# Second graph convolution: gathers a chunk ahead, loads behind the picks, node work in smaller steps

## Chip, cores and metric

The kernel runs on one core of a Trainium2 chip, in one launch. The metric is the device time of an execution in microseconds. Five runs before the change gave 1869.61 to 1880.85 us, median 1875.18.

The engines, with the names that the profile uses: TensorE is PE (its weight loads are PEld), VectorE is DVE, ScalarE is ACT, GpSimd is POOL, SyncE is SP. Each engine works through its own queue of instructions in order; they meet at semaphores.

## What is computed

Two graph layers over 6250 nodes and 100000 edges, which arrive sorted by destination. The first is a two-step graph convolution (GCN), the second an attention layer; behind each stands a residual sum and a layer norm.

```python
def gcn_conv(x, src, dst, ew, W, b):
    deg = segment_sum(ew, dst); dinv = where(deg > 0, rsqrt(deg), 0)
    norm = dinv[src] * ew * dinv[dst]
    h = x @ W
    return segment_sum(h[src] * norm[:, None], dst) + b
...
h = relu(gcn_conv(x, src, dst, ew, W1, b1))      # with self-loops
h = sigmoid(gcn_conv(h, src, dst, ew, W2, b2))   # the second convolution
x = layernorm(x + h)
...
z = x @ fc_w.T
e = leaky(z[src] @ aw[0] + z[dst] @ aw[1] + (r_h @ fc_r_w.T) @ aw[2])
alpha = softmax of e over the edges of a destination
out = relu(segment_sum(alpha * (z[src] + r_h @ fc_r_w.T), dst) + z @ loop_w)
x = layernorm(x + out)
```

The change touches the stage that computes the second convolution. The same stage finishes the first layer for nodes whose sums are complete, prepares what the attention layer needs of them, and computes the part of the scores that comes from the edges' features.

## The kernel before

The edges are cut into 49 chunks of 2048. Since edges are sorted, the destinations of a chunk lie in a window of 144 nodes, and each chunk advances by about 128 nodes. A chunk's source rows come in two ways. For most of them, 12 groups of rows, `pick` copies rows of a table held on chip (`hot`, in three bf16 parts) with matmuls by a 0/1 mask (L513), and ACT scales the result into `got` (L520). For the rest, 5 groups, POOL starts one indirect DMA each from the table `g2` in memory into `far` (L524). By a manual dependency (L527) a gather waits until the second of the three groups of picks is done. `sum_masks` builds `wm`, the 0/1 matrices that send rows to nodes of the window: DVE writes them for the picked rows (L545) and a small `fb` for the gathered ones (L551), which ACT scales (L560). `scatter` (L569) multiplies all 17 groups with them into one window in PSUM, and `add_in` (L574) has DVE add it into the accumulator `acc2`.

The loop over the chunks (L1157 to L1170) stands under a manual schedule, so each engine gets its instructions in the order in which the program writes them. In round c, SP is given the mask of chunk c + 2 (`load_mask`, L1049, 384 KB, three buffers) and the edge features of chunk c + 1 (`load_chunk`, L964, 768 KB, two buffers); then come the picks of c, its gathers and masks, the scatter of chunk c - 1, the product and sum over the features of chunk c on DVE (`dots_of`, L953 and L954), and the sum of chunk c - 1's window. Loads on SP wait in order, each for its buffer.

Between these stand two places in a round for node work (`pieces.go(ready, 1)`): one behind the masks, one behind `dots_of`. A piece is four blocks of 128 nodes, `x1_of`, a generator that stops at every `yield`; a piece begins when the chunks have passed its nodes. Its steps before the change are: product with `dinv` (L337) and sigmoid (L413); transposes (L417) and sum into `xt` (L419); statistics (L384, L385) and root (L388); reciprocals (L390, L391), norm on ACT (L394) and a store; transposes back (L427) and copy to `x1T` (L428); product with `wfT` (L436), copies to `zrows` (L439) and `asd` (L440) and a store; product with `wfl` (L444) and copies (L445, L449); three parts on DVE (L452 to L454) and a store. That is eight steps, two a round, so a piece fills four rounds. `Pieces` issues the next piece's loads (`xt`, `dr`) when a piece begins. The tiles `mm` in PSUM, which the node work's matmuls write, have two buffers, and they are shared with `row_work`, a second generator that prepares index rows for the attention layer and moves one step a round (L1166).

Of the kernel before, what the change touches and what calls it, by code (L numbers as in the profile page):

```python
# [31 lines left out]
GS = 5  # L32
# [8 lines left out]
def gnn_kernel(ctx, tc, x, src, dst, ea, ew, W1, b1, W2, b2, fcw, fcrw, attn, loopw, out):  # L41
# [11 lines left out]
    nc = tc.nc  # L53
    N, D = x.shape
# [13 lines left out]
    NC = CF + 1  # L68
    assert 9 <= NC <= 64

    batches, c0 = [], 0
    while c0 < NC:
        n = min((2, 5)[len(batches)] if len(batches) < 2 else 7, NC - c0)
# [3 lines left out]
    GP = N // P // 4  # L77
# [23 lines left out]
    edges = ctx.enter_context(ExitStack())  # L101
# [5 lines left out]
    g2 = dram.tile([N, D], F32, name="g2")  # L107
# [4 lines left out]
    masks = dram.tile([NC, P, GP * P], BF16, name="masks")  # L112
# [53 lines left out]
    behind = const.tile([P, P], F32, name="behind")  # L166
# [50 lines left out]
    last = keep.tile([P, NT, P], BF16, name="last")  # L217
# [178 lines left out]
    def whole(some, b0):  # L396

        n = sum(nb == P for _, nb in some)
        return [(P, slice(0, n))] * (n > 0) + [(some[-1][1], slice(n, n + 1))] * (n < len(some))

    def x1_of(acc, b0, n, xp, pool, to_hot):


        some = blocks[b0 : b0 + n]
        w = sum(nb for _, nb in some)
        at = slice(b0 * P, b0 * P + w)
        xt = xp.tile([P, 4, D], F32, name="xt")
        load_some(nc.sync, xt, x, b0, n)
        scale = by_dinv(acc, b0, n, xp)
        next(scale)  # L410
        yield
        next(scale, None)
        nc.scalar.activation(acc[:, at], acc[:, at], AF.Sigmoid, bias=cols[:, 1:2])  # L413
        yield
        ps = pool.tile([P, 4, D], F32, name="mm")
        for b, nb in some:
            nc.tensor.transpose(ps[:nb, b - b0, :], acc[:, b * P : b * P + nb], ident)  # L417
        for p, k in whole(some, b0):
            nc.vector.tensor_add(xt[:p, k, :], xt[:p, k, :], ps[:p, k, :])  # L419
        yield  # L420
        yield from normed(xt, some, b0, xp)
        store_blocks(nc.sync, x1d, xt, b0, n)
        yield
        x1T = xp.tile([P, 512], F32, name="x1T")
        ps = pool.tile([P, 512], F32, name="mm")
        for b, nb in some:
            nc.tensor.transpose(ps[:, (b - b0) * P : (b - b0) * P + nb], xt[:nb, b - b0, :], ident[:nb, :nb])  # L427
        nc.scalar.copy(x1T[:, :w], ps[:, :w])  # L428
        yield
        st = xp.tile([P, 4, D], F32, name="zrows")  # L430
        for k0 in range(0, len(some), 2):
            two = some[k0 : k0 + 2]
            ps = pool.tile([P, 2, D + 2], F32, name="mm")
            for b, nb in two:
                k = b - b0 - k0
                nc.tensor.matmul(ps[:nb, k, :], x1T[:, (b - b0) * P : (b - b0) * P + nb], wfT, start=True, stop=True)  # L436
            for p, k in whole(two, b0 + k0):
                to = slice(k0 + k.start, k0 + k.stop)
                nc.scalar.copy(st[:p, to, :], ps[:p, k, :D])  # L439
                nc.vector.tensor_copy(asd[:p, b0 + to.start : b0 + to.stop, :], ps[:p, k, D:])  # L440
        store_blocks(nc.sync, zd, st, b0, n)
        yield
        ps = pool.tile([P, 512], F32, name="mm")
        nc.tensor.matmul(ps[:, :w], wfl, x1T[:, :w], start=True, stop=True)  # L444
        nc.scalar.copy(acc[:, at], ps[:, :w])  # L445
        if to_hot and b0 < BP:
            m = min(n, BP - b0)
            part = xp.tile([P, 4, 3, D], BF16, name="part", bufs=1)
            nc.scalar.copy(part[:, :m, 0, :], st[:, :m])  # L449
            yield  # L450
            left = xp.tile([P, 4, D], F32, name="low")[:, :m]
            nc.vector.tensor_sub(left, st[:, :m], part[:, :m, 0, :])  # L452
            nc.vector.tensor_copy(part[:, :m, 1, :], left)
            nc.vector.tensor_sub(part[:, :m, 2, :], left, part[:, :m, 1, :])  # L454
            nc.sync.dma_start(hz[:, b0 : b0 + m], part[:, :m])
# [45 lines left out]
            while left:  # L501
                left = [piece for piece in left if next(piece, self) is not self]

    def pick(c, mask, hot, table, ps_g, wp, gots=4, fars=12):

        rows = []
        for g0 in range(0, GP, 4):
            n = min(4, GP - g0)
            ps = ps_g.tile([P, 4, D], F32, name="g")
            for g in range(n):  # L510
                for k in range(3):
                    for q in range(4):
                        picked = nc.tensor.matmul(ps[32 * q : 32 * q + 32, g, :],  # L513
                                         mask[:, (g0 + g) * P + 32 * q : (g0 + g) * P + 32 * q + 32],
                                         hot[:, 4 * (g0 + g) + q, k, :], start=k == 0, stop=k == 2)
            if g0 + 8 <= GP:
                most = picked
            got = wp.tile([P, 4, D], F32, name="got", bufs=gots)
            for g in range(n):
                nc.scalar.activation(got[:, g, :], ps[:, g, :], AF.Copy, scale=swt[:, c, g0 + g : g0 + g + 1])  # L520
            rows += [got[:, g, :] for g in range(n)]
        for g in range(GS):
            got = wp.tile([P, D], F32, name="far", bufs=fars)
            brought = nc.gpsimd.indirect_dma_start(  # L524
                out=got, out_offset=None, in_=table[:, :],
                in_offset=bass.IndirectOffsetOnAxis(ap=sidx[:, c, g : g + 1], axis=0))
            tc.add_manual_dep(brought.ins, most.ins.name,  # L527
                              mybir.DependencyInfo(mybir.DependencyClass.Sync, mybir.DependencyReason.DATA),
                              reason="rows by DMA behind most of a chunk's picks")
            rows.append(got)  # L530
        return rows

    def sum_masks(c, wp, halved=True, nears=2):

# [37 lines left out]
    def add_in(acc, c, ps):  # L572
        at = cbase_of(c)
        nc.vector.tensor_add(acc[:, ds(at, WC)], acc[:, ds(at, WC)], ps)  # L574
# [9 lines left out]
    with tc.tile_pool(name="prep", bufs=1) as prep, tc.tile_pool(name="ps_p", bufs=3, space=PSUM) as ps_mm, \  # L584
# [115 lines left out]
        ps = ps_mm.tile([P, 4, D], F32, name="mm")  # L700
# [12 lines left out]
    hot = hotp.enter_context(tc.tile_pool(name="hot", bufs=1)).tile([P, BP, 3, D], BF16, name="hot")  # L713
# [4 lines left out]
    sorts, c0 = [], 0  # L718
    while c0 < NC:
        n = min((3, 4)[len(sorts)] if len(sorts) < 2 else BATCH, NC - c0)  # L720
# [187 lines left out]
    with tc.tile_pool(name="xs0", bufs=1) as xp, tc.tile_pool(name="ps_d", bufs=3, space=PSUM) as ps_mm, \  # L908
# [8 lines left out]
        with tc.high_priority():  # L917
            for c0 in range(0, NC, 7):
                n = min(7, NC - c0)
# [3 lines left out]
                for c in range(c0, c0 + n):  # L923
                    m = ms[:, c - c0]
                    ps = ps_w.tile([3, WC], F32, name="win")
# [10 lines left out]
            ps = ps_w.tile([P, NB], F32, name="win")  # L936
# [16 lines left out]
            nc.vector.tensor_mul(part, part, ar_row[:p, None, None, :].to_broadcast([p, *part.shape[1:]]))  # L953
            nc.vector.tensor_reduce(dots[:p, c : c + m, ts], part, AX.X, OP.add)  # L954

    def load_edges(et, c0, n, ts):

        for c in range(c0, c0 + n) if c0 + n > CF else [c0]:
            m = 1 if c0 + n > CF else n
            cuts = [(0, P)] if c < CF else [(0, 96), (96, crem // TC)]  # L960
            for p0, p1 in cuts:
                of = ea[c * CC : min((c + m) * CC, c * CC + (p1 * TC if c == CF else m * CC)), :]
                of = of.rearrange("(c p t) f -> p c t f", c=m, t=TC)
                nc.sync.dma_start(et[p0:p1, c - c0 : c - c0 + m], of[p0:p1, :, ts, :])  # L964

    def early_dots(pool):

# [75 lines left out]
    kp = first.enter_context(tc.tile_pool(name="slots2", bufs=3))  # L1043
    slots_of = {}

    def load_mask(c):
        if c < NC:
            slots_of[c] = kp.tile([P, GP * P], BF16, name="mask")
            nc.sync.dma_start(slots_of[c], masks[c])  # L1049

    load_mask(0)
    load_mask(1)
    ap_ = edge_rows.enter_context(tc.tile_pool(name="arp", bufs=2))
    ets = {}

    def load_chunk(c):
        if c < NC:
            ets[c] = ap_.tile([P, 1, TL, D], F32, name="et")
            load_edges(ets[c], c, 1, slice(0, TL))

    load_chunk(0)
    with tc.tile_pool(name="tab2", bufs=2) as wp, tc.tile_pool(name="ps_t", bufs=3, space=PSUM) as ps_mm:
# [7 lines left out]
    with tc.tile_pool(name="conv2", bufs=2) as wp, tc.tile_pool(name="rows2", bufs=1) as rp, tc.tile_pool(name="x1p", bufs=2) as xp, \  # L1070
# [79 lines left out]
        rows_of = row_work()  # L1150

        nc.gpsimd.memset(asd, 0.0)
        pieces = Pieces(lambda b0, n: x1_of(acc2, b0, n, xp, ps_mm, True))
        held = None

        with tc.manual_schedule():
            for c in range(NC):  # L1157
                ready = lows[max(c - 1, 0)]
                load_mask(c + 2)
                load_chunk(c + 1)  # L1160
                new = pick(c, slots_of.pop(c), hot, g2, ps_g, wp, 6), sum_masks(c, wp, halved=False)
                pieces.go(ready, 1)
                if held is not None:
                    win = scatter(held, ps_w)
                dots_of(ets.pop(c), c, 1, slice(0, TL))
                next(rows_of, None)  # L1166
                pieces.go(ready, 1)
                if held is not None:
                    add_in(acc2, c - 1, win)
                held = new  # L1170
            for _ in rows_of:
                pass
            load_mask(0)
            load_mask(1)
            add_in(acc2, NC - 1, scatter(held, ps_w))
            pieces.finish()
# [473 lines left out]
```

## Time and profile before

| | us |
|---|---|
| median of five runs | 1875.18 |
| the profiled execution | 1876.59 |
| its span | 1874.7 |
| PE busy (matmuls) | 1509.3 (81% of the span) |
| DVE busy | 1409.0 (75%) |
| ACT busy | 1111.5 (59%) |
| POOL busy | 912.4 (49%) |

The span is the time from the first to the last instruction that the profiler recorded. A table of groups gives, for each line, engine and operation, its busy time and the mean of one; a table of waits says for which engine and line an instruction waited, with the total, how often and the longest. "issue" there means that the engine waited for nothing that the profile shows. In a timeline a row is a start, a duration, the engine, the line, the operation with its tiles and a count of merged instructions; in brackets stands the idle time before it and what ended it. The granted clock of PE, a share of full speed, was 0.908 over the profiled execution. Since neighbouring instructions overlap in the pipelines, a busy PE is not necessarily at its peak.

### The profile page before, as it was taken

The numbers are of one execution on the slowest core, as the hardware profiler recorded it, in microseconds if no ns is written. First come the engines' busy times: TensorE is split into PE (matmuls) and PEld (weight loads), VectorE is DVE, ScalarE is ACT, GpSimd is POOL, SyncE is SP. The second block draws the span as 40 slices with busy tenths as digits, with TensorE's granted clock in tenths as the row PEclk, the third lists the DMA queues.
The fourth block names the chain that finished last, engine by engine and source line by source line (L and its number), as shares of the span: only waits on it lengthen the run. The fifth ranks groups of instructions, "written<-read, shape, count | busy, mean of one in ns | idle before, by whom it ended". The sixth has DMA issues, their size and how long they took to land.

```text
span 1874.7 us, 77963 instructions
## 1 busy us (share of the span) xinstructions
PE 1509.3 (81%) x33767; PEld 1376.4 (73%) x33767; DVE 1409.0 (75%) x2979; ACT 1111.5 (59%) x3537; POOL 912.4 (49%) x951
## 2 busy tenths in 40 slices
PE   2866888989998777888989986578888788888996
PEld 1554787888997657777878875467778777788885
DVE  7695878887776578877887874788887777877552
ACT  1135565667788654667767764235666656667774
POOL 4023454566576447766776762114334344344552
PEclk9987999999998868899999997569999999999998
DMA  2112333344458666666776675655667567676663
GB/s 61 42 38 85 100 112 101 108 131 135 135 156 262 198 188 188 196 208 203 225 236 197 214 218 177 188 146 158 206 169 219 156 187 195 181 205 171 178 199 72
DMA packets 261369, 306.86 MB, mean 164 GB/s; under 512 B 38387, under 2 KB 193785, under 8 KB 260212
## 3 DMA queue, kind: packets, MB, share of 16 engines
q1 hardware_dynamic: 229311, 244.90, 41.5%
q0 software_dynamic: 23520, 48.22, 12.4%
q10 hardware_dynamic: 8184, 8.65, 1.4%
q8 instruction: 267, 4.37, 1.0%
q14 instruction: 87, 0.71, 0.1%
HBM read 260.42 MB, written 41.25 MB: 161 GB/s over the span
## 4 chain that ended last, share of the span: by engine, by line
PE 26%; DMA 12%; DVE 11%; issue 7%; POOL 6%; ACT 3%; SPq 0%; DVEq 0%; POOLq 0%; ACTq 0%
PE win L569 11%; POOL far L524 6%; PE g L513 6%; DMA rk<-srow 4%; DMA far<-g,sidx 4%; PE r L1414 2%; PE k L1267 2%; DMA al<-shd 2%; DVE sel L1270 1%; PE mm L362 1%; ACT got L520 1%; DVE wb L265 1%; DVE ohm L265 1%; PE rec L1431 1%; DVE asr L1271 1%
## 5 line engine op out<-in xcount | busy, mean ns | idle before, releaser
L524 POOL DMA_INDIRECT far<-g,sidx x490 | 581.5, 1187 | 332.7 <-PE g L513 174.2
L520 ACT ACTIVATE got<-g,swt 128x128 f32<-128x128 f32 x1764 | 484.2, 386 | 249.2 <-PE g L513 196.5
L569 PE MATMUL win<-wm,got 128*128 128x144 f32 x3528 | 499.6, 300 | 11.8 <-issue 9.6
L569 PEld LDWEIGHTS win<-wm,got 128*128 128x128 f32 x3528 | 472.1, 200 | 28.4 <-issue 21.7
L524 POOL DMA_INDIRECT far<-zd,sidx x245 | 268.1, 1094 | 440.1 <-PE g L513 346.6
L513 PE MATMUL g<-hot,mask 128*32 128x128 bf16 x21168 | 373.8, 228 | 67.3 <-issue 58.8
L513 PEld LDWEIGHTS <-mask 128*32 128x32 bf16 x21168 | 326.9, 101 | 95.4 <-issue 80.5
L560 ACT ACTIVATE wm<-fb,swt 128x64 f32<-128x64 bf16 (+1 forms) x735 | 198.7, 384 | 43.7 <-DVE swt L1386 28.2
L569 PE MATMUL win<-wm,far 128*128 128x64 f32 (+1 forms) x1470 | 186.4, 272 | 29.0 <-DMA far<-g,sidx 29.0
L569 PEld LDWEIGHTS win<-wm,far 128*128 128x128 f32 x1470 | 181.4, 194 | 31.5 <-issue 21.7
L543 ACT CAST wm<-wb 128x864 f32<-128x864 bf16 x196 | 177.4, 953 | 23.5 <-PE win L569 18.7
L1267 PE MATMUL k<-adp,rk 128*128 128x49 bf16 x2352 | 89.7, 194 | 53.2 <-DVE sel L1270 46.9
L574 DVE TENSOR_TENSOR acc<-acc,win 128x144 f32 x147 | 44.4, 302 | 115.0 <-PE win L569 105.0
L1267 PEld LDWEIGHTS <-rk 128*128 128x128 bf16 x2352 | 83.1, 103 | 62.8 <-issue 51.2
L265 DVE TENSOR_TENSOR ohm<-iotab,pm 128x2048 bf16<-128x2048 bf16 x98 | 118.9, 1213 | 1.6 <-PE rec L849 1.5
L265 DVE TENSOR_TENSOR wb<-iota,sdst 128x1728 bf16<-128x1728 bf16 x98 | 103.0, 1051 | 19.4 <-ACT wm L543 19.3
L351 POOL TENSOR_TENSOR hot<-low,hot 128x512 bf16<-128x512 f32 x24 | 37.4, 1558 | 136.0 <-DVE hot L350 123.6
L545 DVE TENSOR_TENSOR wm<-iota,sdst 128x1728 f32<-128x1728 f32 x49 | 95.6, 1951 | 1.1 <-POOL hot L351 1.1
L954 DVE TENSOR_REDUCE dots<-et 128x12 f32<-128x1536 f32 (+1 forms) x49 | 85.9, 1753 | 1.7
L953 DVE TENSOR_TENSOR et<-et,ar_row 128x1536 f32<-128x1536 f32 (+1 forms) x49 | 85.6, 1747 | 0.0
L1259 DVE TENSOR_SCALAR rk<-rk,iotap 128x1024 bf16<-128x1024 bf16 x98 | 48.1, 494 | 36.5 <-DMA rk<-srow 36.2
L1262 ACT COPY blk<-blks 128x16 bf16<-128x16 bf16 x98 | 19.5, 207 | 92.9 <-DVE ohb L265 89.1
(401 smaller groups left out, 2259.9 us busy)
## 6 DMA issues: line engine op xcount, KB each, us to landing
et<-in_edge_attr_dram SPq DMA_DIRECT2D x97, 512.0 KB
mask<-masks SPq DMA_DIRECT2D x98, 384.0 KB
et<-in_edge_attr_dram SPq DMA_DIRECT2D x48, 768.0 KB
rk<-srow SPq DMA_DIRECT2D x98, 256.0 KB
mask<-srd SPq DMA_DIRECT2D x49, 384.0 KB
masks<-mask SPq DMA_DIRECT2D x49, 384.0 KB
ee<-in_edge_attr_dram SPq DMA_DIRECT2D x24, 512.0 KB
far<-g,sidx POOLq DMA_INDIRECT x490
```

Of the source, the lines that this page charges most:

```text
L265: nc.vector.tensor_tensor(out.rearrange("p t (h d) -> p t h d", d=2), row[:, None].to_broadcast(some), of[:, :, None, :].to_broadcast(some ...
L513: picked = nc.tensor.matmul(ps[32 * q : 32 * q + 32, g, :], mask[:, (g0 + g) * P + 32 * q : (g0 + g) * P + 32 * q + 32], hot[:, 4 * (g0 + ...
L520: nc.scalar.activation(got[:, g, :], ps[:, g, :], AF.Copy, scale=swt[:, c, g0 + g : g0 + g + 1])
L524: brought = nc.gpsimd.indirect_dma_start(out=got, out_offset=None, in_=table[:, :], in_offset=bass.IndirectOffsetOnAxis(ap=sidx[:, c, g : ...
L543: nc.scalar.copy(wm[:, n0 : n0 + half], wb[:, n0 : n0 + half])
L545: nc.vector.tensor_tensor(wm[:, :NEAR].rearrange("p (g w) -> p g w", w=WC), iota[:, None, 1 : WC + 1].to_broadcast([P, GP, WC]), sdst[:, c ...
L560: nc.scalar.activation(m, b, AF.Copy, scale=swt[:, c, GP + g : GP + g + 1])
L569: nc.tensor.matmul(ps[:, n0 : n0 + m.shape[-1]], row, m, start=g == 0, stop=g == len(rows) - 1)
L953: nc.vector.tensor_mul(part, part, ar_row[:p, None, None, :].to_broadcast([p, *part.shape[1:]]))
L954: nc.vector.tensor_reduce(dots[:p, c : c + m, ts], part, AX.X, OP.add)
L1259: nc.vector.tensor_scalar(mk, mk, iotap, None, op0=OP.is_equal)
L1267: nc.tensor.matmul(ps[:, s, :], mk[:, s * P : (s + 1) * P], adp[:, 0, k, :NB], start=k == 0, stop=k == 2)
```

## The change

Three things change, all in the second convolution's stage.

The first is the order of the gathers. `pick` is cut into `picks` and `bring`. The third stage and the first convolution still call them together, with the same dependency. In the second convolution, chunk 0's gathers are issued ahead of the loop without a dependency on picks, and in round c the gathers of chunk c + 1 are issued behind the second group of picks of chunk c. The tile `far` gets 15 buffers instead of 12.

The second is where the loads stand: `load_mask(c + 2)` and `load_chunk(c + 1)` are issued after the picks of chunk c in the program, and each of them gets a dependency on the last matmul of these picks.

The third is the node work. `apart()` is a further stop in `x1_of` between a group of matmuls and the operations of other engines that read their result. There are four of them, so a piece has twelve steps; a third `pieces.go(ready, 1)` stands at the end of a round, behind `add_in`. While a piece stops at such a place it holds tiles `mm` (`turns["held"]`), and `row_work` does not move. The two products with `wfT` are now both issued before the copies of the first. After the loop the stops are off.

```diff
-    def x1_of(acc, b0, n, xp, pool, to_hot):
+    def x1_of(acc, b0, n, xp, pool, to_hot, turns=None):
+
+        def apart():
 
+            if turns and not turns["last"]:
+                turns["held"] = True
+                yield
+                turns["held"] = False
...
             nc.tensor.transpose(ps[:nb, b - b0, :], acc[:, b * P : b * P + nb], ident)
+        yield from apart()
...
             nc.tensor.transpose(ps[:, (b - b0) * P : (b - b0) * P + nb], xt[:nb, b - b0, :], ident[:nb, :nb])
+        yield from apart()
         nc.scalar.copy(x1T[:, :w], ps[:, :w])
...
                 nc.tensor.matmul(ps[:nb, k, :], x1T[:, (b - b0) * P : (b - b0) * P + nb], wfT, start=True, stop=True)
+            twos.append((k0, two, ps))
+        yield from apart()
+        for k0, two, ps in twos:
...
         nc.tensor.matmul(ps[:, :w], wfl, x1T[:, :w], start=True, stop=True)
+        yield from apart()
         nc.scalar.copy(acc[:, at], ps[:, :w])
...
+    def bring(c, table, wp, fars, mark=None):
+
+        rows = []
         for g in range(GS):
             got = wp.tile([P, D], F32, name="far", bufs=fars)
             brought = nc.gpsimd.indirect_dma_start(
                 out=got, out_offset=None, in_=table[:, :],
                 in_offset=bass.IndirectOffsetOnAxis(ap=sidx[:, c, g : g + 1], axis=0))
-            tc.add_manual_dep(brought.ins, most.ins.name,
...
+            if mark is not None:
+                behind_of(brought, mark, "rows by DMA behind most of a chunk's picks")
...
+    def pick(c, mask, hot, table, ps_g, wp, gots=4, fars=12):
+
+        rows, marks = picks(c, mask, hot, ps_g, wp, gots)
+        return rows + bring(c, table, wp, fars, marks[-2])
...
-        pieces = Pieces(lambda b0, n: x1_of(acc2, b0, n, xp, ps_mm, True))
+        turns = {"held": False, "last": False}
+        pieces = Pieces(lambda b0, n: x1_of(acc2, b0, n, xp, ps_mm, True, turns))
...
         with tc.manual_schedule():
+            far = bring(0, g2, wp, 3 * GS)
             for c in range(NC):
                 ready = lows[max(c - 1, 0)]
-                load_mask(c + 2)
-                load_chunk(c + 1)
-                new = pick(c, slots_of.pop(c), hot, g2, ps_g, wp, 6), sum_masks(c, wp, halved=False)
+                rows, marks = picks(c, slots_of.pop(c), hot, ps_g, wp, 6)
+                new = rows + far, sum_masks(c, wp, halved=False)
+                if c + 1 < NC:
+                    far = bring(c + 1, g2, wp, 3 * GS, marks[-2])
+                load_mask(c + 2, marks[-1])
+                load_chunk(c + 1, marks[-1])
                 pieces.go(ready, 1)
                 if held is not None:
                     win = scatter(held, ps_w)
                 dots_of(ets.pop(c), c, 1, slice(0, TL))
-                next(rows_of, None)
                 pieces.go(ready, 1)
+                if not turns["held"]:
+                    next(rows_of, None)
                 if held is not None:
                     add_in(acc2, c - 1, win)
+                pieces.go(ready, 1)
                 held = new
+            turns["last"] = True
+            while turns["held"]:
+                pieces.go(N, 1)
```

More of the change, by code (lines that the diff above doesn't have):

```diff
@@ L430, in x1_of @@
         st = xp.tile([P, 4, D], F32, name="zrows")
+        twos = []
         for k0 in range(0, len(some), 2):
@@ L502, in finish, with behind_of, picks @@
                 left = [piece for piece in left if next(piece, self) is not self]
-    def pick(c, mask, hot, table, ps_g, wp, gots=4, fars=12):
-        rows = []
+    def behind_of(instruction, mark, reason):
+        tc.add_manual_dep(instruction.ins, mark.ins.name,
+                          mybir.DependencyInfo(mybir.DependencyClass.Sync, mybir.DependencyReason.DATA), reason=reason)
+    def picks(c, mask, hot, ps_g, wp, gots):
+        rows, marks = [], []
         for g0 in range(0, GP, 4):
@@ L515, in pick @@
                                          hot[:, 4 * (g0 + g) + q, k, :], start=k == 0, stop=k == 2)
-            if g0 + 8 <= GP:
-                most = picked
+            marks.append(picked)
             got = wp.tile([P, 4, D], F32, name="got", bufs=gots)
@@ L521, in pick @@
             rows += [got[:, g, :] for g in range(n)]
+        return rows, marks
+    def bring(c, table, wp, fars, mark=None):
+        rows = []
         for g in range(GS):
@@ L526, in pick @@
                 in_offset=bass.IndirectOffsetOnAxis(ap=sidx[:, c, g : g + 1], axis=0))
-            tc.add_manual_dep(brought.ins, most.ins.name,
-                              mybir.DependencyInfo(mybir.DependencyClass.Sync, mybir.DependencyReason.DATA),
-                              reason="rows by DMA behind most of a chunk's picks")
+            if mark is not None:
+                behind_of(brought, mark, "rows by DMA behind most of a chunk's picks")
             rows.append(got)
         return rows
+    def pick(c, mask, hot, table, ps_g, wp, gots=4, fars=12):
+        rows, marks = picks(c, mask, hot, ps_g, wp, gots)
+        return rows + bring(c, table, wp, fars, marks[-2])
     def sum_masks(c, wp, halved=True, nears=2):
@@ L954, in dots_of, with load_edges @@
             nc.vector.tensor_reduce(dots[:p, c : c + m, ts], part, AX.X, OP.add)
-    def load_edges(et, c0, n, ts):
+    def load_edges(et, c0, n, ts, mark=None):
         for c in range(c0, c0 + n) if c0 + n > CF else [c0]:
@@ L963, in load_edges @@
                 of = of.rearrange("(c p t) f -> p c t f", c=m, t=TC)
-                nc.sync.dma_start(et[p0:p1, c - c0 : c - c0 + m], of[p0:p1, :, ts, :])
+                brought = nc.sync.dma_start(et[p0:p1, c - c0 : c - c0 + m], of[p0:p1, :, ts, :])
+                if mark is not None:
+                    behind_of(brought, mark, "edges' features behind a chunk's picks")
     def early_dots(pool):
@@ L1044, in gnn_kernel, with load_mask @@
     slots_of = {}
-    def load_mask(c):
+    def load_mask(c, mark=None):
         if c < NC:
             slots_of[c] = kp.tile([P, GP * P], BF16, name="mask")
-            nc.sync.dma_start(slots_of[c], masks[c])
+            brought = nc.sync.dma_start(slots_of[c], masks[c])
+            if mark is not None:
+                behind_of(brought, mark, "slots' masks behind a chunk's picks")
     load_mask(0)
@@ L1054, in gnn_kernel, with load_chunk @@
     ets = {}
-    def load_chunk(c):
+    def load_chunk(c, mark=None):
         if c < NC:
             ets[c] = ap_.tile([P, 1, TL, D], F32, name="et")
-            load_edges(ets[c], c, 1, slice(0, TL))
+            load_edges(ets[c], c, 1, slice(0, TL), mark)
     load_chunk(0)
```

## The prediction

> **What bounds it now.** The page's table of groups says which work belongs to the change: the gathers (L524) into `far`, the matmuls that take them (L569), the picks (L513). The start times of L545 (once a chunk) place the second convolution: 49 chunks from 696.9 to 1149.7 us, and between 710.5 and 1133.0 us 47 chunks, 8.99 us each. Next, busy time of each engine in that stretch:
>
> ```profile
> core 0: us, PE busy (x) PEld busy (x) DVE busy (x) ACT busy (x) POOL busy (x), PEclk, DMA share, GB/s
> 710.50:1133.00 422.50, 356.53 (x8387) 332.25 (x8378) 341.81 (x437) 286.40 (x929) 299.91 (x232) 0.93 0.69 208
> ```
>
> TensorE (PE) is busy 84%, VectorE (DVE) 81%: neither is a bound by work alone. So, the waits of the same stretch, by engine (us in all, times, longest):
>
> ```profile
> PE g L513 <- issue: 37.4, 20, 4.0
> PE win L569 <- DMA far<-g,sidx: 20.8, 11, 5.2
> PE mm L427 <- ACT xt L394: 2.1, 1, 2.1
> ...
> DVE xt L419 <- PE mm L417: 24.6, 11, 4.6
> DVE asd L440 <- ACT zrows L439: 20.2, 15, 5.1
> DVE acc L574 <- PE win L569: 9.6, 7, 2.3
> ```
>
> PE's busy time and its waits (37.4, 20.8 and some 7 small ones) fill 422 us: PE never rests for another reason, and DVE's waits are mostly for PE. PE's order sets the pace, with two stalls: gathered rows that land late, and "issue" inside the picks. I counted matmuls between successive "issue" stalls in the timeline: 255, 128, 128, 128, 252 where they follow closely, multiples of about 128 elsewhere (some records are missing). 128 matmuls with 128 weight loads are 256 instructions, so these are refills of PE's instruction stream, which travel by DMA:
>
> ```profile
> q8 instruction: 267, 4.37, 1.0%
> ```
>
> 4.37 MB in 267 packets is 16 KB each. The longest stalls follow bursts on the load queue. From 969.35 to 975.27 us SyncE (SP) issued mask, edge rows, xt, dr, mask, edge rows: 2816 KB in 6 us, 470 GB/s asked where 208 flow; the refill stall behind it is the first row below.
>
> ```profile
> 982.47 0.52 PE L513 MATMUL g<-hot,mask 128*32 128x128 bf16 x24 [3.81 <-issue]
> 982.92 4.88 PE L569 MATMUL win<-wm,got 128*128 128x144 f32 x24
> ...
> 991.41 3.11 PE L569 MATMUL win<-wm,got 128*128 128x144 f32 x24
> ```
>
> The same 24 matmuls take 4.88 us after the pause and 3.11 otherwise: a pause is paid a second time by a slow clock.
>
> **The four-chunk cycle.** A piece of node work (four blocks) lasts four chunks. From 749.83 to 1132.87 us are 42 chunks, 9.12 each, so 36.5 us a cycle. Undisturbed chunks of each kind last (L545 to L545) 8.2 (product, transposes, xt sum), 8.1 (statistics, norm), 8.2 (transposes, zrows) and 7.6 (loop product, parts): 32.1. Stalls thus cost 4.4 a cycle.
>
> **The change, part by part.** No computing instruction is added; order and waits change.
>
> *Gathers one chunk ahead.* The same five L524 a chunk, on the otherwise empty POOL queue, behind the same place in the picks, but for the next chunk. A gather's time to its use grows by a chunk of 8 to 9 us; the longest landing pieces in the chain of waits are 7.4 to 8.5 us. So the 20.8 us go, with the slow clock behind them. POOL itself needs 5 x (1.29 + 0.30) = 7.9 us a chunk, 32 a cycle: under the new cycle below, it does not bind. At the end, chunk 48's last rows held PE 0.39 + 1.41 + 2.78 us (from 1143.7):
>
> ```profile
> 1149.10 0.61 PE L569 MATMUL win<-wm,far 128*128 128x16 f32 x2 [2.78 <-DMA far<-g,sidx]
> ```
>
> These 4.6 us go. At the head (chunks 0 to 5) the wait of 5.2 us at 716.7 and the slow picks behind it (4.03 against 2.2) go in part, since POOL is busy back to back there in both: I take 4, bounds 0 and 7.
>
> *Masks and features behind the picks.* One 384 KB and one 768 KB load a chunk wait on SP for the last pick; behind them in SP's queue stand xt, dr and the stores of the node work, none of which is wanted within a chunk. Two pairs can no longer be sent within 6 us, so refills meet a shorter queue. Lead of the edge rows: end of picks to the next L953 is 8.5 us or more in the cycle below, less 0.4 of issue; the shortest lead in the trace without a DVE wait is 7.4 (714.66 to 722.02). Cost 0; were a load to land as late as the longest gather (8.5), one chunk in four would wait 0.4, some 4 us in all. The cover is one chunk of DVE work; without it, the whole landing would stand before every L953.
>
> *Node work cut.* Eight steps become twelve, three a chunk, again exactly a piece in four chunks. The third place comes after DVE's sum into acc. Row work is only put off. The cut adds one order that matters: the norm on ScalarE (ACT, L394) is now step 5 and the transposes that read it (L427) step 6, the next place of the **same** chunk, where before a whole set of picks lay between. In the trace:
>
> ```profile
> 977.72 1.95 DVE L545 TENSOR_TENSOR wm<-iota,sdst 128x1728 f32<-128x1728 f32 x1
> 983.19 1.75 DVE L954 TENSOR_REDUCE dots<-et 128x12 f32<-128x1536 f32 x1
> 987.47 1.65 ACT L394 ACTIVATE xt<-xt,rs 128x128 f32<-128x128 f32 x4 [0.44 <-DVE rs L391]
> 988.79 2.19 PE L513 MATMUL g<-hot,mask 128*32 128x128 bf16 x144
> 990.91 0.66 PE L427 MATMUL mm<-ident,xt 128*128 128x128 f32 x4
> ```
>
> DVE ends L954 7.2 us after L545; reciprocals (0.35), semaphore and norm (1.65) end at 9.2. PE began its picks 0.9 before L545 and needs 2.2 + 4.3 for picks and scatter: done at 5.7. Then it now waits for the norm, its four transposes following the four norms, until 9.5. Queued behind: the next picks, so ACT's `got`, the next scatter, and DVE's next sum into acc.
>
> Write D for a chunk's L545 start, p for its picks' start. First kind: DVE 6.2 to the end of the dots, sum into acc 0.5, xt sum 0.7, so 7.4; PE leaves 1.1 before the next D. Second: DVE 8.1 as now; PE leaves at D + 9.5, 1.4 **after** the next D. Third: picks 2.2, scatter 4.3, wfT 1.1, so the next p is 7.6 on; DVE's asd copies wait for the zrows copies until p + 8.4 = D + 9.8. Fourth (p 0.8 before D): picks 2.2, loop product 1.1, scatter 4.4 end at D + 6.9; sum 0.5, then the parts 1.85, now behind the sum instead of before it: 9.3. Total 34.6 a cycle undisturbed, against 32.1: **the cut costs 2.5**.
>
> To this come two surcharges. *Clock*: PE's pause is 2.4 us (5.7 to 8.1, first transpose). The nearest row is the same wait seen once:
>
> ```profile
> 771.19 1.63 PE L427 MATMUL mm<-ident,xt 128*128 128x128 f32 x4 [2.06 <-ACT xt L394]
> 772.61 4.35 PE L569 MATMUL win<-wm,got 128*128 128x144 f32 x24
> ```
>
> 4.35 against 3.11 is +1.2, which I take; bounds 0 and 1.8 (slow picks after 5.2 us, 4.03 against 2.2). [...] *Refills*: 37.4 us over 47 chunks are 0.8 a chunk; two chunks of the four (third and fourth) have PE on the path, so 1.6 if nothing improves, 0 if all go. Without bursts I take 0.3. [...]
>
> Sum: 34.6 + 1.2 + 0.3 = 36.1 a cycle against 36.5, over 42 / 4 = 10.5 cycles -4.2 us; tail -4.6; head -4. Together -12.8. The profiled execution took 1876.6 (span 1874.7 and 1.9 around it), 1.4 over the median of 1875.2. So 1863.8 there, **1862** beside the median. All gains at their bounds: 34.6 a cycle, -20.0 - 4.6 - 7 = -31.6, 1844. All losses: 38.0 a cycle, +15.8 - 4.6 = +11.2, 1886.
>
> **Rivals.** A run can tell 0.5% (9.4 us) from no change.
>
> *The norm's wait decides (slower).* The mechanism is L427 behind L394 on PE, once in four chunks; it turns the balance once the two surcharges exceed 2.7 us a cycle (36.5 - 34.6 + 8.6 / 10.5). With clock 1.8 and refills 1.6 it gives 1886. For it: PE is the full engine, and every pause over 2 us that I looked at was followed by slow matmuls. Against: refill stalls in the first two kinds now fall into slack, and bursts end. Chance 0.34.
>
> *It comes out even*, surcharges of 1.8 to 3.6 and head and tail as above: within 9.4 us, say 1874. For it: the terms are as large as the sum. Chance 0.22.
>
> *The wait is covered* (much faster): if PE lags DVE for other reasons when it gets to L427, only the old stalls vanish: cycle 33, -36.8 - 8.6, 1830. For it: the undisturbed chunks of now; against: it needs PE late by 3.8 us in each statistics chunk. Chance 0.08.
>
> *Gathers bind POOL*: beside L545 and L953 a gather takes 1.6 to 2.2 us, alone 0.94. With all five at 1.8 + 0.3, 10.5 a chunk, 42 a cycle, +58 us, 1933; but in an 8.2-us chunk three of the five fall outside. Chance 0.02, counted with slower.
>
> Forecast (modest gain): 0.34; with the covered case, faster 0.42, same 0.22, slower 0.36. The forecast's own range is 1844 to 1866; the whole one, 1836 to 1892, takes in the bounds and the rivals, and leaves out most of the covered case and a slower one with late loads.
>
> **What would show it.** Right: waits of L569 for `far` near 0 until 1140 us; L427 waiting 2 to 4 us for L394 in eleven pieces (25 to 40 us in all, now 2.1); "issue" at L513 under 20 us; L545 about every 9.0 us, in the pattern 7.4, 8.1, 9.8, 9.3 and more. Wrong: L427 without a wait (then 1830); DVE waiting for `et` at L953; POOL without idle time; "issue" as before. It fails altogether if the third and fourth kinds keep their 8.2 and 7.6.

## The result and the profile after

The changed kernel took 1873.1 us (median; 1862.7 to 1888.7) against 1876.6 for the kernel before beside it: ratio 0.9982, 95% interval 0.9969 to 0.9995. The forecast was 1862. The profiled execution of the changed kernel has a span of 1871.9 us at a mean granted clock of 0.908, against 1874.7 at the same clock: 2.8 us gained where 12.8 were expected.

The busy times and the chief waits of PE and DVE in the changed kernel in the stretch from 710.5 to 1133.0 us, the same as shown for before:

```profile
core 0: us, PE busy (x) PEld busy (x) DVE busy (x) ACT busy (x) POOL busy (x), PEclk, DMA share, GB/s
710.50:1133.00 422.50, 363.90 (x8577) 336.06 (x8570) 346.35 (x439) 292.26 (x948) 313.08 (x244) 0.94 0.69 210
```

```profile
DVE acc L600 <- PE win L595: 49.6, 26, 4.7
PE g L531 <- issue: 17.8, 11, 3.7
PE mm L434 <- ACT xt L394: 12.4, 7, 2.4
PE mm L423 <- ACT acc L419: 12.4, 11, 2.9
DVE asd L452 <- ACT zrows L451: 8.3, 18, 0.6
PE win L595 <- DMA far<-g,sidx: 7.4, 2, 3.7
```

The stalls that the change aimed at have shrunk: "issue" at the picks from 37.4 to 17.8 us, the wait for gathered rows from 20.8 to 7.4, and these 7.4 lie before 724 us. Two waits are new or larger on PE, each of 12.4 us: the second transposes for the norm (L434, was 2.1) and the first transposes for the sigmoid (L423), which was short before:

```profile
PE mm L417 <- ACT acc L413: 1.8, 3, 1.0
```

DVE waits less for node work (1.8 us for the first transposes at `xt`, was 24.6; 8.3 at `asd`, was 20.2) and more for PE's sum of a window (49.6 at `acc`, was 9.6).

The starts of the masks (L545, now L571) show where the time went. Row four counts from the start of chunk 6 to that of chunk 48.

| us | before | changed | difference |
|---|---|---|---|
| first mask of the stage | 696.9 | 707.5 | +10.6 |
| mask of chunk 6 | 749.8 | 759.5 | +9.7 |
| mask of chunk 48 | 1132.9 | 1131.6 | -1.3 |
| these 42 chunks | 383.0 | 372.1 | -10.9 |
| last sum into acc | 1149.7 | 1143.3 | -6.5 |
| end of the span | 1874.7 | 1871.9 | -2.8 |

So the loop became faster by 10.9 us, more than forecast, and the end of the stage (last mask to last sum) by 5.2. What is missing was lost before chunk 6 (9.7 us) and behind the last sum (3.7 us). The head of the stage in the timeline of before:

```profile
696.91 1.96 DVE L545 TENSOR_TENSOR wm<-iota,sdst 128x1728 f32<-128x1728 f32 x1 [1.05 <-POOL hot L351]
697.63 2.07 POOL L524 DMA_INDIRECT far<-g,sidx  x1 [0.76 <-PE g L513]
...
708.72 0.69 DVE L954 TENSOR_REDUCE dots<-ee 106x4 f32<-106x512 f32 x1
```

And after the change:

```profile
706.62 0.69 DVE L980 TENSOR_REDUCE dots<-ee 106x4 f32<-106x512 f32 x1
707.50 1.96 DVE L571 TENSOR_TENSOR wm<-iota,sdst 128x1728 f32<-128x1728 f32 x1 [0.19 <-DMA et<-in_edge_attr_dram]
707.55 3.21 ACT L537 ACTIVATE got<-g,swt 128x128 f32<-128x128 f32 x12 [12.17 <-DMA et<-in_edge_attr_dram]
708.14 2.15 POOL L546 DMA_INDIRECT far<-g,sidx  x1 [10.90 <-DMA et<-in_edge_attr_dram]
...
719.63 0.64 PE L595 MATMUL win<-wm,far 128*128 128x64 f32 x2 [3.71 <-DMA far<-g,sidx]
723.96 0.66 PE L595 MATMUL win<-wm,far 128*128 128x64 f32 x2 [3.69 <-DMA far<-g,sidx]
```

`ee` are the edge features of a stretch of work that ends here: DVE sums over them (`early_dots`). Before, the new stage began 12.5 us ahead of the end of the last of these sums, and DVE did both in turn. After, ACT, DVE and POOL all begin within 0.9 us of the end of the last sum, POOL after 10.9 us of idle time. A `far` gather needs no data of the early sums. The rows name a load as releaser (`et`, issued at 703.2 us), but neither the masks nor a gather reads `et`. The reading that the experiments below test is that the stage waited for memory: in the changed program's layout the stage's pool ends at byte 178304 of a partition and `ee` begins at byte 178176. With 12 buffers of `far` the pool ends at 176768, with 14 at 177792. The fifteenth buffer makes 128 bytes of the pool coincide with a tile of the early sums. The gathers of chunks 0 and 1 then stand on POOL back to back from 708 to 725 us, and PE waits twice for them.

### The profile page after: what moved, and what is told of

Read it like the earlier page. It is cut to its first block, busy times and chain, and to the rows that moved or that the text cites. A ratio compares the mean times of both kernels' runs of the same rounds, so it can differ in the third digit from the quotient of the medians.

```text
span 1871.9 us, 77961 instructions
## 1 busy us (share of the span) xinstructions
PE 1503.3 (80%) x33767; PEld 1367.4 (73%) x33767; DVE 1408.3 (75%) x2979; ACT 1112.2 (59%) x3537; POOL 914.8 (49%) x951
## 3 DMA queue, kind: packets, MB, share of 16 engines
q0 software_dynamic: 23520, 48.22, 12.5%
## 4 chain that ended last, share of the span: by engine, by line
PE 32%; DVE 15%; DMA 9%; ACT 5%; issue 4%; POOL 0%; SPq 0%; DVEq 0%; ACTq 0%
PE win L595 13%; PE g L531 8%; DMA rk<-srow 5%; PE k L1307 2%; PE r L1454 2%; DVE wm L571 2%; PE mm L362 1%; DVE sel L1310 1%; DMA dk<-drow 1%; DVE wb L265 1%; ACT wm L586 1%; DVE ohm L265 1%; ACT L419 1%; DVE dots L980 1%; PE rec L1471 1%
## 5 line engine op out<-in xcount | busy, mean ns | idle before, releaser
L595 PE MATMUL win<-wm,got 128*128 128x144 f32 x3528 | 488.4, 296 | 10.4 <-issue 9.8
L595 PEld LDWEIGHTS win<-wm,got 128*128 128x128 f32 x3528 | 460.1, 196 | 28.5 <-issue 22.0
L531 PEld LDWEIGHTS <-mask 128*32 128x32 bf16 x21168 | 331.3, 102 | 86.6 <-issue 70.4
L595 PE MATMUL win<-wm,far 128*128 128x64 f32 (+1 forms) x1470 | 182.0, 270 | 12.9 <-DMA far<-g,sidx 11.9
L595 PEld LDWEIGHTS win<-wm,far 128*128 128x128 f32 x1470 | 178.7, 192 | 13.6 <-issue 13.6
L571 DVE TENSOR_TENSOR wm<-iota,sdst 128x1728 f32<-128x1728 f32 x49 | 95.9, 1957 | 0.2 <-DMA et<-in_edge_attr_dram 0.2
```

The source lines that it names most:

```text
L531: picked = nc.tensor.matmul(ps[32 * q : 32 * q + 32, g, :], mask[:, (g0 + g) * P + 32 * q : (g0 + g) * P + 32 * q + 32], hot[:, 4 * (g0 + ...
L571: nc.vector.tensor_tensor(wm[:, :NEAR].rearrange("p (g w) -> p g w", w=WC), iota[:, None, 1 : WC + 1].to_broadcast([P, GP, WC]), sdst[:, c ...
L595: nc.tensor.matmul(ps[:, n0 : n0 + m.shape[-1]], row, m, start=g == 0, stop=g == len(rows) - 1)
```

## The experiments

In four of the five sets of runs every kernel, the one before included, took about 20% longer (the kernel before 2222 to 2289 us; one chip gave 1877 in one set and 2283 in another). So each ratio is against the kernel before of its own set, and "set at 1877" is the one that compares with the result.

**The late start.** The kernel before with 15 buffers of `far` and nothing else, and the changed kernel with 14:

```diff
-                new = pick(c, slots_of.pop(c), hot, g2, ps_g, wp, 6), sum_masks(c, wp, halved=False)
+                new = pick(c, slots_of.pop(c), hot, g2, ps_g, wp, 6, 15), sum_masks(c, wp, halved=False)
```

> The kernel before with one number changed: 15 buffers of far instead of 12. Theory A (the start of the stage pays for the extra memory): in the changed kernel the pool of the second convolution is 1536 bytes a partition longer, its fb tile then ends at byte 178304, and the tiles ee of the early dots begin at 178176; by these 128 bytes the whole pool waits for the last early dots. Then this kernel starts its first wm at about 707 us instead of 697 and is 6 to 10 us slower than before (ratio 1.003 to 1.005). Theory B (the gathers put ahead of the loop, or the loads behind picks, delay the start): more buffers alone do nothing, first wm at 697 us, ratio 0.998 to 1.002.

```diff
-            far = bring(0, g2, wp, 3 * GS)
+            far = bring(0, g2, wp, 3 * GS - 1)
...
-                    far = bring(c + 1, g2, wp, 3 * GS, marks[-2])
+                    far = bring(c + 1, g2, wp, 3 * GS - 1, marks[-2])
```

> The changed kernel with 14 buffers of far instead of 15: fb ends at byte 177792, 384 bytes short of ee. Theory A: the first wm starts at about 697 us as in the kernel before, everything behind it comes about 9 us earlier, and the time is 1863 to 1867 us where the changed kernel has 1873 (ratio to before 0.992 to 0.995). The fifth gather of a chunk then waits for a scatter that has long run, which costs nothing. Theory B: first wm at 707 us, time as the changed kernel's, ratio 0.997 to 0.999.

The timeline of the kernel before with 15 buffers:

```profile
824.60 0.69 DVE L954 TENSOR_REDUCE dots<-ee 106x4 f32<-106x512 f32 x1
825.47 1.96 DVE L545 TENSOR_TENSOR wm<-iota,sdst 128x1728 f32<-128x1728 f32 x1 [0.19 <-DVE dots L954]
826.20 2.06 POOL L524 DMA_INDIRECT far<-g,sidx  x1 [10.03 <-DVE dots L954]
```

The size of `far` alone reproduces the late start in a kernel without any other part of the change, and here the row names the early sum as the releaser. Over all traces it is without exception: in the six with 15 buffers the first mask starts 0.2 us after the last early sum; in the fourteen with 12 or 14 it starts 12.5 to 14.1 us before that sum ends. A load that lands late is excluded as the cause, since the kernel before with 15 buffers has its loads where they were. The times of the same runs disagree about the price. In one set 15 buffers gave 1.0117 (1.0057 to 1.0177) on the kernel before, and with the norm's stop moved (next experiment) 1.0132 where 14 gave 0.9975. In another set they gave 1.0018 (0.9974 to 1.0062) on the kernel before. The changed kernel gave 1.0256 (1.0210 to 1.0301) with 15 and, in other sets, 1.0254, 1.0249 and 1.0300 with 14. These sets took over 2200 us, where 10 us are little against another loss of 2.5%. The last repeat too fell in such a set, though its forecast is for 1877:

> The changed kernel with 14 buffers of far in place of 15, beside a kernel before that takes about 1877 us. Theory A (the 128 shared bytes hold the start back by 10 us and the sixth chunk by as much): first wm at 692 to 698 us, sixth chunk starts 6 to 10 us earlier than in the changed kernel; 1862 to 1868, ratio 0.992 to 0.996. Rival (DVE has the early sums to do in any case): ratio 0.997 or more.

**The stop for the norm.** In the changed kernel the second transposes follow the norm in the same round. This edit moves the stop from behind them to ahead of them, so that they come a place later and a set of picks lies between:

```diff
         store_blocks(nc.sync, x1d, xt, b0, n)
         yield
+        if turns and not turns["last"]:
+            yield
         x1T = xp.tile([P, 512], F32, name="x1T")
...
             nc.tensor.transpose(ps[:, (b - b0) * P : (b - b0) * P + nb], xt[:nb, b - b0, :], ident[:nb, :nb])
-        yield from apart()
         nc.scalar.copy(x1T[:, :w], ps[:, :w])
```

> The changed kernel with the node work's second transposes one place later: an empty stop between the norm on ACT and the transposes, and none between the transposes and the copy that follows them; still twelve steps. Theory A (the transposes stand behind a norm that has not run, and the next picks behind them): PE's wait for the norm, 12.4 us in 7 waits between 710 and 1133 us, goes to under 4; chunks of the third kind go from 9.4 to about 8.3 us, a cycle of four from 35.4 to 34 to 34.8, the time down by 6 to 14 us (ratio to before 0.990 to 0.995). Theory B (PE has slack there): the pattern of the four kinds and the time stay within 3 us of the changed kernel's.

With 14 buffers as well:

> Both edits: 14 buffers of far, and the second transposes one place later. If both causes are real and stand apart, the gains add: 1851 to 1861 us, ratio 0.986 to 0.991. If only the memory matters: 1863 to 1867. If neither: 1873.

In the sets over 2200 us, with the stop as changed: 1.0254, 1.0249, 1.0256 and 1.0300, third kind of chunk 13.0, 12.9, 13.6 and 13.1 us in the mean. With the stop moved: 1.0132 (1.0065 to 1.0199) with 15 buffers, and 0.9975, 1.0021, 0.9990 and 0.9987 (0.9958 to 1.0016) with 14, third kind 9.0, 8.8, 8.1, 8.3 and 8.3. The changed kernel by itself was among these runs:

> The changed kernel as it is, beside the kernel before on whatever chip these runs fall. Theory A (PE's stop for the norm decides wherever PE's instructions come slowly): where the kernel before takes about 1876 us, ratio 0.997 to 1.000 and a stop of PE for the norm under 2.5 us; where it takes over 2200 us, ratio 1.015 to 1.03, stops for the norm of 4 us and more, and third kinds of chunk of 13 us mean or more. Rival (the loss seen there belongs to the 14 buffers of far, whose fifth gather has to wait for the chunk before the last to be used up): ratio 0.995 to 1.005 there too, and third kinds under 11 us.

In three sets the kernels with 14 buffers differ in the stop alone, and moving it takes the loss away. So the loss of 2.5% there is the norm's stop; the fourteen buffers are cleared. The changed kernel's timeline in such a set has a chunk of 17.2 us behind a stop of 2.4 (1117.59 to 1134.81):

```profile
1117.61 1.63 PE L434 MATMUL mm<-ident,xt 128*128 128x128 f32 x4 [2.39 <-ACT xt L394]
1119.16 4.03 PE L531 MATMUL g<-hot,mask 128*32 128x128 bf16 x144
...
1120.75 2.42 ACT L537 ACTIVATE got<-g,swt 128x128 f32<-128x128 f32 x8 [2.04 <-PE g L531]
1123.12 3.94 PE L595 MATMUL win<-wm,got 128*128 128x144 f32 x24
...
1129.35 1.14 ACT L537 ACTIVATE got<-g,swt 128x128 f32<-128x128 f32 x4 [6.18 <-PE win L595]
1129.87 0.31 DVE L600 TENSOR_TENSOR acc<-acc,win 128x144 f32 x1 [6.63 <-PE win L595]
1132.19 2.10 PE L445 MATMUL mm<-wfT,x1T 128*128 128x130 f32 x8 [2.37 <-ACT x1T L436]
1134.22 3.92 PE L531 MATMUL g<-hot,mask 128*32 128x128 bf16 x144
```

The picks behind the stop take 4.03 us instead of 2.2 and end at 1123.2. ACT gets to the last four scalings only at 1129.35, its copy of x1T comes behind them, PE waits for that (2.37), and the next picks are slow again (3.92). The longest single piece of the chunk is the 6.2 us in which ACT waits, and why it waits so long wasn't found.

The same order alone on the kernel before, in the set at 1877 (the loop's lines are shown; in the generator a flag is set behind the norm, and a further stop stands behind the copy to `x1T`, so the first place of the next round stays empty and a piece still fills four rounds):

```diff
                     add_in(acc2, c - 1, win)
+                if turns["more"]:
+                    turns["more"] = False
+                    pieces.go(ready, 1)
```

> The kernel before with one step moved: the second transposes of a piece, which read the norm, are issued behind the sum into acc of the norm's own round, and the first place of the next round stays empty. Loads, gathers and all other steps as before. Theory A (this order alone makes the loss): where the kernel before takes over 2200 us, ratio 1.015 to 1.03; where it takes 1876 us, 1.003 to 1.015. PE waits 2 to 4.5 us for the norm some ten times. Rival (the loss needs the other stops or the third place too): ratio 0.995 to 1.007.

1890.6 us, ratio 1.0076 (1.0050 to 1.0103): slower by 13 us, with loads, gathers and the other steps as before. PE waits for the norm 9.2 us in 7 pieces, longest 2.9, less than the ten waits of 2 us and more that were forecast, and the third kind of chunk goes from 9.2 to 11.1 us in the mean. So the order alone costs, without the other stops and the third place.

**Wait or clock.** The changed kernel with matmuls that need nothing, ahead of the second transposes (overwritten by them):

```diff
+        if turns and not turns["last"]:
+            for _ in range(12):
+                nc.tensor.matmul(ps[:, :P], ident, ident, start=True, stop=True)
```

> The changed kernel with twelve matmuls (128x128, f32, of the identity, overwritten by the transposes) ahead of the second transposes of a piece: they wait for nothing and keep PE busy for about 2.6 us of the stop. Theory C (the stop itself is covered; it is the slow matmuls behind it that cost): the picks behind the transposes take 2.2 us again instead of 3.4 to 4.0, the third kind falls from 13.5 us to under 11, the time from 1.025 to 1.005 or less of the kernel before. Rival D (the place of the norm and of what waits for it in ACT's and DVE's queues costs, whatever the clock): third kinds stay over 12.5 us, ratio 1.02 or more.

The same step of the first piece, first in the changed kernel, then with the matmuls:

```profile
776.50 1.63 PE L434 MATMUL mm<-ident,xt 128*128 128x128 f32 x4 [2.40 <-ACT xt L394]
778.07 3.62 PE L531 MATMUL g<-hot,mask 128*32 128x128 bf16 x144
```

```profile
772.58 2.90 PE L435 MATMUL mm<-ident 128*128 128x128 f32 x24
775.31 1.32 PE L437 MATMUL mm<-ident,xt 128*128 128x128 f32 x4
776.56 2.19 PE L534 MATMUL g<-hot,mask 128*32 128x128 bf16 x144
```

With the pause filled the picks take 2.19 to 2.23 us in all nine pieces whose picks the trace holds as one group. In the changed kernel they take 2.82 in the mean of ten such, and 3.1 to 3.6 behind three stops of 2.35 to 2.40. The granted clock shows it directly: in the changed kernel it is 0.50 from 777.7 to 781.1 us, while the slow picks above run, and 1.00 from 850.9 to 853.1 us, where picks take 2.19. So the clock fell behind this pause of 2.40 us. It is not the norm's doing alone: two more of the ten took 3.7 us at a mean granted clock of 0.55 and 0.56, the first behind a stop for the norm of 0.82 us and the second behind none, where PE had waited 2.70 us for row work. The time does not follow: 1878.6 us, ratio 1.0007 (0.9985 to 1.0029), and the third kind of chunk stayed at 9.8 us. The matmuls take 2.9 us or more in every piece, also where PE came late and would not have waited, so this run does not part the price of the stop from that of filling it.

**What the parts are worth without the stop.** Two kernels in the set at 1877 have the stop moved. One has the gathers ahead (14 buffers) and the loads at the start of a round as before:

```diff
+                load_mask(c + 2)
+                load_chunk(c + 1)
                 rows, marks = picks(c, slots_of.pop(c), hot, ps_g, wp, 6)
...
-                load_mask(c + 2, marks[-1])
-                load_chunk(c + 1, marks[-1])
```

> The kernel with both stops mended (14 buffers of far, the stop moved), and masks and features loaded at the start of a round without a dependency, as before the change. Theory A (the loads' place is worth refill stalls of PE): slower than the kernel with both mended (0.9975 to 1.002) by 0.3 to 1 per cent. Rival (the refills cost the same wherever the loads stand): the same within 0.3 per cent.

The other has the loads behind the picks and the gathers as before (12 buffers):

```diff
-            far = bring(0, g2, wp, 3 * GS)
...
-                new = rows + far, sum_masks(c, wp, halved=False)
-                if c + 1 < NC:
-                    far = bring(c + 1, g2, wp, 3 * GS, marks[-2])
+                new = rows + bring(c, g2, wp, 12, marks[-2]), sum_masks(c, wp, halved=False)
```

> The kernel with the stop moved and the gathers behind their own chunk's picks in 12 buffers, as before the change. Theory A (gathers ahead gain on the way and at the end): waits of PE for far 15 us or more in the stage, last wm to last sum 4 us longer, slower than the kernel with both mended by 0.4 to 1.3 per cent (1.003 to 1.015 of before). Rival: the same within 0.3 per cent.

The first took 1847.0 us, ratio 0.9845 (0.9821 to 0.9869): 30 us under the kernel before and the fastest of all kernels run. The second took 1863.0, ratio 0.9923 (0.9895 to 0.9950). The two differ in the gathers and in the loads' place, so the 16 us between them are not the gathers' alone. Waits of PE in the stretch from 710.5 us, first with gathers ahead, then with gathers as before:

```profile
PE g L532 <- issue: 25.6, 18, 5.9
PE mm L423 <- ACT acc L419: 16.2, 13, 3.1
...
PE win L596 <- DMA far<-g,sidx: 4.3, 1, 4.3
```

```profile
PE win L596 <- DMA far<-g,sidx: 21.0, 15, 3.5
PE g L532 <- issue: 14.7, 12, 3.3
PE mm L423 <- ACT acc L419: 12.8, 10, 3.1
```

Without gathers ahead the wait for rows is back at the 21 us of before, and the end of the stage, last mask to last sum, takes 16.9 us as before, against 11.1 with them. No wait for the norm is left in either, and the third kind of chunk is 7.8 and 8.4 us in the mean. The same step of the first piece, with picks between norm and transposes:

```profile
765.33 2.30 PE L532 MATMUL g<-hot,mask 128*32 128x128 bf16 x144
767.12 1.65 ACT L394 ACTIVATE xt<-xt,rs 128x128 f32<-128x128 f32 x4 [1.25 <-DVE rs L391]
...
767.67 1.48 PE L436 MATMUL mm<-ident,xt 128*128 128x128 f32 x4
```

From the mask of chunk 6 to that of chunk 48 the two need 355.7 and 363.8 us, against 383.0 before and 372.1 in the changed kernel, and chunk 6 starts at 751.5 and 744.2 against 759.5. (The profiled executions of the two took 1851.1 and 1853.5 us, nearer to each other than the medians.)

All three parts with the stop moved and 14 buffers were run only in sets over 2200 us. The last of these runs, with its forecast for 1877:

> Gathers ahead in 14 buffers, loads behind the picks, node work cut with the stop ahead of the second transposes: the change with both stops mended, on a chip where the kernel before takes about 1877 us. Theory A (the loads' place saves refill stalls): issue at the picks under 18 us in the stage, against 25.6 with the loads as before, and 4 to 12 us less than with these (1847): 1835 to 1843, ratio 0.978 to 0.982. Rival (the loads' place is worth nothing, as issue moves elsewhere): 1843 to 1852, ratio 0.982 to 0.987.

It gave 0.9987 beside 2283 us, no gain, as the same kernel did three times before. So the loads' place stays open. "Issue" at the picks was 17.8 and 14.7 us with the loads behind the picks, and 25.6 with the loads as before; but it was 24.6 in the kernel with the filling matmuls, whose loads also stand behind the picks, and no pair of runs differs in the loads alone.

**Two that told little**, both in sets over 2200 us. Node work in eight steps as before, with the other two parts and 14 buffers, gave 0.9956 (0.9881 to 1.0032) and 1.0015 (0.9978 to 1.0052), the same as the whole with the stop moved:

> 14 buffers of far, gathers ahead and loads behind the picks as in the change, but node work in eight steps with two places a round as before the change. Theory A (gathers and loads gain some 2 us a cycle each, the cut of the node work gives it back): the kinds of chunk come near 8.2, 8.1, 8.2, 7.6 us, waits of PE for far under 8 us and issue under 20 in the stage, cycle 32.5 to 34; 1838 to 1855, ratio 0.980 to 0.989. Theory B (the first kind's fall from 9.8 to 7.3 us is the work of the cut, which took DVE's waits for PE away): the first kind stays at 9 us or more, cycle 35.5 to 37, time 1866 or more, ratio 0.995 to 1.003.

The ratios and first kinds of 10.5 and 11.6 us lie where theory B put them, but the whole with the stop moved has the same ratios and first kinds of 9.4 to 10.7 there, so the cut shows neither gain nor cost once its stop is moved. In the set with 1.0015 the changed kernel gave 1.0256: without the cut its loss is gone. The changed kernel with only the gathers as before gave 1.0187 (1.0119 to 1.0255) beside 1.0256, which the intervals can't part:

> The changed kernel with each chunk's gathers behind its own picks and 12 buffers again; loads and node work as changed. Theory A (gathers ahead gain 2 us a cycle and 5 us at the end): PE waits for far 15 us or more in the stage again, the end of the stage (last wm to last sum) is 15 us or more, and the time is 0.3 to 1.5 per cent over the kernel with both stops mended (14 buffers, stop moved); the start of the stage is not held back. Rival (gathers ahead are worth nothing on the way, since PE stands for the norm anyway): waits for far under 8 us without the gathers ahead, time within 0.3 per cent of the changed kernel.

## Why the prediction was wrong

**The step that failed** reads: "At the head (chunks 0 to 5) the wait of 5.2 us at 716.7 and the slow picks behind it (4.03 against 2.2) go in part, since POOL is busy back to back there in both: I take 4, bounds 0 and 7." Chunk 6 began 9.7 us later instead of 4 earlier: a miss of 13.7 us, more than the whole gap between the gain forecast (12.8) and the one measured (2.8). The prediction counted the three further buffers of `far` at nothing and never asked what lay in those bytes before. The bounds held no loss, though nothing excluded one. What the runs showed in its place: with 15 buffers the first mask starts 0.2 us after the last early sum, in all six traces; with 12 or 14 it starts 12.5 to 14.1 us before that sum ends, in all fourteen. Its price, 8 to 15 us by the start of chunk 6 (759.5 against 751.5 and 744.2), is not shown by itself; it is read from traces of kernels that differ in other things too.

**Gathers ahead** were forecast to end the 20.8 us of waits: 7.4 are left, all at the head, and the kernel without the part has 21.0. Right.

**Loads behind the picks** were taken at no cost, with "issue" under 20. It fell to 17.8, with 4.3 more at L595; DVE waited once for `et`, 1.9 us. The signs are as forecast, but "issue" fell to 25.6 with the loads as before too, so what their place is worth stays open. Of the matmuls counted between "issue" stalls, the sequence in the prediction (255, 128, 128, 128, 252) does not come out of the trace as it stands; in the stretch the counts at the picks are 253, 384, 382, 512 and so on, multiples of about 128 as it says. That these stalls are refills of PE's instructions is the author's inference from such counts and from the instruction queue, whose 267 packets for 67534 matmuls and weight loads make 253 each; for the end of such a stall the waits name nothing but "issue".

**The cut of the node work** was forecast in the pattern 7.4, 8.1, 9.8, 9.3 us. The four kinds had means of 7.3, 9.3, 9.4, 9.5 and minima of 7.0, 8.1, 7.3, 8.7. The norm's stop was seen rightly, a pause of 2.4 us, but in seven pieces and not eleven (12.4 us where 25 to 40 were expected); in the other four PE came to the transposes after the norm. The clock surcharge of 1.2 us a cycle was 0.6 (2.82 against 2.19) in the picks. In the kernel before, the scatter that it was taken from (4.35 us at 772.61) ran at a granted clock of 0.71, the one of 4.88 us behind "issue" (982.92) at 0.65 and the one of 3.11 (991.41) at 1.00. Put at nothing: PE's wait for the sigmoid ahead of the first transposes, 12.4 us in eleven waits. The cut did not add this order, since both kernels issue the sigmoid at a round's first place and the transposes at its second; before, PE waited there 1.8 us in three. Why the wait grew isn't shown. Together the cycle took 35.4 us (372.1 / 10.5) instead of 36.1, so the loop gave 10.9 where 4.2 were forecast.

**The tail** was right at its place, -5.2 against -4.6, and did not reach the end: from the last chunk's mask to the end of the span the kernels need 741.8 (before), 740.3 (changed), 742.0 and 743.7 (gathers ahead, and as before, with the stop moved), and 741.6 (norm's stop alone). Behind the last sum the five take 724.9 to 731.0 us, 3.7 more in the changed kernel than before; the prediction put a difference there at nothing, and its cause stays open.

**The rivals.** "The norm's wait decides" names a cost that is there: 13 us where the order stands alone, and 2.5% of the changed kernel in the sets over 2200 us. In the main measurement its condition did not hold, since the loop took 35.4 us a cycle and gained. "It comes out even" is what the main measurement gave, but for another reason than the surcharges it named. "The wait is covered" (1830 us, cycle 33) is nearest to the kernel with gathers ahead, the stop moved and the loads as before: 1847 us, cycle 33.9.

The sums close roughly: 30 us from gathers ahead and the cut with its stop moved, less 13 for the stop as it is and 8 to 15 for the start, leave 2 to 9 of gain, where 3.5 were measured. That is worked out from different kernels, with the loads' place counted at nothing, and not shown.

## What to carry to other kernels

When a change adds buffers to a pool, look up what lived in those bytes: here a pool that overlapped a still-used tile by 128 bytes started 0.2 us after the last sum that reads the tile, where without the overlap it had started 12.5 us before that sum's end. When node work is cut finer, list every pair of steps that now lies within a round without other work of PE between, and put the longest chain of other engines (statistics, root, norm) where a set of matmuls covers it: here that one order cost 13 us by itself, and 2.5% in the sets over 2200 us. Test a change in more than one set of runs; its sign differed between them.

## What was not expected of the hardware

The same program on the same chip took 1877 us in one set and 2283 in another. The waits of PE over the whole span, first of the kernel before at 1876.6 us, then of the same with 15 buffers at 2246:

```profile
PE g L513 <- issue: 58.8, 39, 4.1
...
PE win L569 <- issue: 9.6, 9, 3.0
```

```profile
PE r L1414 <- issue: 71.9, 195, 1.4
PE g L513 <- issue: 58.8, 109, 2.0
PE win L569 <- issue: 47.5, 94, 1.8
```

In the longer run PE pauses far more often without a wait that the profile shows: 94 times, 1.8 us at most, within the scatter alone, where it was 9. The mean granted clock is 0.871 instead of 0.908. In that condition the norm's stop costs about twice its waits: in the three sets that have both kernels with 14 buffers, the loop from chunk 6 to 48 takes 472 to 484 us with the stop and 419 to 425 with it moved, and PE's waits for the norm are 28 to 32 us. Why the condition differs between sets wasn't found. Nor was it found why ACT's last scalings there start up to 6 us after the picks that they read.
